# Denominators that leave PSUM group by group, four PSUM banks used in turn, and an order chosen among ten

## The chip, the cores and the metric

The kernel runs on one core of one Trainium2 chip. The metric is the device time of one execution in microseconds (us). The kernel before took 819.15, 821.52 and 824.37 us in three executions; their median is 821.52 us. A further execution was profiled; its own time stands in the table below.

## The reference

The computation is one pre-norm layer over `x` of 4 batches, 512 tokens and 1024 features, in float32:

```
h    = layernorm(x)
q    = h @ Wq                         # 32 heads of 32
k, v = split(h @ Wkv)                 # one key head and one value head for all 32 query heads
s    = q k^T / sqrt(32) + slope[head] * (key - query), causal
x    = x + softmax(s) v @ Wo
w    = (unpack6(qweight) - zero_point) * scale          # 1024 x 1024, four 6-bit codes per 3 words
x    = x + layernorm(x) @ w^T + bias
```

Softmax is computed as exp(s - max) with the products against the values first and the division by the sum of the exponentials (the denominator) later.

## The kernel before

**Tiling.** The 32 heads are taken as 8 groups of 4 heads, for each of 4 batches: 32 steps. A step of the attention runs through these stages; the names in quotes are the tiles that the profile prints.

- `queries` (matmuls on L703 into "pq"): 24 matmuls of 512 columns; the weights and the normalised input are split into a high and a low part, so three products per chunk. ScalarE copies the high part "qh", VectorE subtracts to get the low part "ql", both go through DRAM ("q_d") and come back stacked by head in "qs", of which there are three buffers.
- `maxima` (L762 into "s", two PSUM banks): scores with queries on partitions; VectorE takes each row's maximum (L778, "junk", "mx"). The maxima are transposed ("trm", L794), split ("mt") and sent by DMA into two rows of "qs".
- `attention` (L846 into "st", two PSUM banks): scores with keys on partitions, the maximum already subtracted by the extra rows; ScalarE exponentiates out of PSUM (L856, "p"), GpSimd clears what lies above the diagonal (L865). The products with the values (L875, "pav") and the denominators (L904, "den") are matmuls of 32 output columns, four of them side by side in the array (`tiled=True` for the planner). Before the denominators GpSimd adds the later key blocks of "p" onto the first (L887). "pav" is copied out by ScalarE (L893, "a") and stored to DRAM ("at_d").
- The denominators of the 8 groups of a batch are added into one PSUM tile "den" with a selecting weight "onesel", so that group g stands in row g of each head's 32 partitions. After the eighth group `invert` (L916) takes the reciprocal of the whole tile in four VectorE instructions and four DMAs store it ("rden_d").

**Afterwards**, for 16 tiles of 128 tokens: "raw" (products and reciprocals fetched from DRAM, multiplied on GpSimd, L1051), the output projection (L1074, "po", 48 matmuls of 512 columns per tile), residual, layernorm, a transposition, and the feed-forward product (L1194, "pf", 32 matmuls per tile). In between, `unpack` turns the packed weights into codes: for each of 8 row blocks a load ("qw"), three VectorE instructions, a transposing DMA and a store.

**PSUM.** There are eight banks: two for "s", two for "st", and one each for four pools. "av" holds "pav", "den" the denominators of a batch, "q" the queries, and "misc" the transposed inputs "tr", the keys and values "pkv", "trkv" and "trm". Towards the end "q" and "misc" also serve "po", "pf" and "tr" of the first token tiles.

**What sets the order.** Nothing is issued as it is written down. Each operation is recorded with an engine, a cost, a due time `at` and the items it reads and writes. `Work.slots` gives each new tile of a pool the buffer whose last use is due first, and adds the edges that follow from the reuse. `Work.forward` then lays all operations out in time, engine by engine, with fixed latencies (`LAT`: the time from the end of an operation until another engine sees it), `Work.backward` derives when each is wanted, and `Work.order` repeats this (four rounds of six passes), keeping the order whose end comes first. The instructions of TensorE, ScalarE, VectorE, GpSimd and the DMA queue of SyncE (SP) stand in that order in the program; each queue is served strictly in order, so an instruction that waits holds all behind it. The token tiles (`token_tile`) and the reuse of "q" and "misc" there are part of the same plan.

## Time and profile before

| | |
|---|---|
| profiled execution: its own time / its span | 821.6 us / 819.6 us |
| median of the three runs | 821.52 us (819.15 to 824.37) |
| TensorE (PE) busy | 796.1 us, 97% |
| PE weight loads (PEld) busy | 592.9 us, 72% |
| VectorE (DVE) busy | 563.6 us, 69% |
| GpSimd (POOL) busy | 520.2 us, 63% |
| ScalarE (ACT) busy | 378.3 us, 46% |
| mean granted PE clock | 0.997 |
| chain that ended last | PE 89%, DVE 4%, ACT 2%, DMA 2%, POOL 2%, issue 1% |
| matmuls recorded: L703 pq / L1074 po / L1194 pf | 768 / 768 / 512, of 512 columns |
| L904 den | 256 records, 33.9 us |
| L916 reciprocals | 16, 937 ns each |
| L893 copy of "pav" | 32, 588 ns each |

The span is the time from the first to the last profiled instruction; some 2 us of the execution lie around it. A PE that is called busy can still lose time: matmuls are pipelined and overlap in the records, so what a matmul costs is read from the distance between the starts of neighbours, not from its own duration. Idle time of an engine is listed with what ended it.

### The profile page before, as it was taken

To read this page: it belongs to the slowest core of one execution; us is meant where nothing else is said; L and a number is where in the kernel's file an instruction comes from. 1 tells how busy PE (TensorE), PEld (TensorE's weight loads), DVE (VectorE), ACT (ScalarE), POOL (GpSimd) and SP (SyncE) were. 2 spreads that over 40 slices of the span, in tenths; PEclk is the share of its full clock that TensorE was granted. 3 is DMA by queue.
4 is the path that set the end of the run, shared out by engine and by line. 5 is a ranking of instruction groups with operands and counts; after the bars stand their busy time and mean duration, and the time that the engine had idled before them with its cause. 6 is when DMAs were issued, how large, how long until landed. Compare 5 with 4: busy or idle time off the path is not lost.

```text
span 819.6 us, 13342 instructions
## 1 busy us (share of the span) xinstructions
PE 796.1 (97%) x4464; PEld 592.9 (72%) x4464; DVE 563.6 (69%) x1496; ACT 378.3 (46%) x669; POOL 520.2 (63%) x442
## 2 busy tenths in 40 slices
PE   5999999999899999999999999999999999999997
PEld 5767666777566777666777677667888888888886
DVE  7576776478767278678457776644997686667755
ACT  5644754655665544786555574340142322323320
POOL 5239876556857554797289997878556444545623
PEclk9999999999999999999999999999999999999999
DMA  7277642566733576954659775446985565567311
GB/s 228 64 178 201 191 140 72 153 186 188 231 91 88 156 198 198 263 148 106 198 166 265 205 224 172 159 108 141 245 183 142 144 166 130 131 142 174 103 39 64
DMA packets 130355, 130.76 MB, mean 160 GB/s; under 512 B 42804, under 2 KB 92980, under 8 KB 129264
## 3 DMA queue, kind: packets, MB, share of 16 engines
q1 hardware_dynamic: 129472, 126.39, 56.0%
q0 software_dynamic: 816, 3.53, 1.6%
q8 instruction: 35, 0.57, 0.3%
q14 instruction: 32, 0.26, 0.1%
HBM read 84.01 MB, written 38.80 MB: 150 GB/s over the span
## 4 chain that ended last, share of the span: by engine, by line
PE 89%; DVE 4%; ACT 2%; DMA 2%; POOL 2%; issue 1%; DVEq 0%; POOLq 0%
PE po L1074 21%; PE pq L703 19%; PE pf L1194 14%; PE st L846 9%; PE s L762 9%; PE pav L875 8%; PE den L904 4%; DVE junk L778 2%; PE tr L602 2%; PE pkv L620 2%; POOL p L887 1%; DMA wo_st<-in_L_attn_Wo_dram 1%; ACT p L856 1%; DVE qs L684 1%; DMA x<-_attn_hidden_states_dram 0%
## 5 line engine op out<-in xcount | busy, mean ns | idle before, releaser
L778 DVE CUSTOM_DVE_ANT_0 junk<-s,mask 128x384 f32<-128x384 f32 (+3 forms) x512 | 250.3, 489 | 118.3 <-PE s L762 90.3
L887 POOL TENSOR_TENSOR p<-p,p 128x1536 f32<-128x1536 f32 (+2 forms) x96 | 231.6, 2412 | 18.7 <-PE pav L875 16.9
L856 ACT ACTIVATE p<-st 128x512 f32<-128x512 f32 (+1 forms) x352 | 184.8, 560 | 111.4 <-PE st L846 99.8
L703 PE MATMUL pq<-xc,wqh 128*128 128x512 f32 x512 | 198.3, 403 | 0.2
L1074 PE MATMUL po<-woh,aT 128*128 128x512 f32 x512 | 166.3, 391 | 0.0
L865 POOL TENSOR_SCALAR_AFFINE_SELECT p<-p 128x512 f32<-128x512 f32 x128 | 83.9, 660 | 117.8 <-ACT p L856 116.3
L762 PE MATMUL s<-kst,qs 124*128 124x384 f32 (+3 forms) x512 | 128.3, 325 | 6.4 <-DVE mx L778 3.1
L846 PE MATMUL st<-qs,kst 126*128 126x512 f32 (+1 forms) x352 | 128.2, 401 | 2.0 <-ACT p L856 1.7
L762 PEld LDWEIGHTS s<-kst,qs 124*128 124x128 f32 x512 | 91.6, 189 | 43.4 <-DVE mx L778 12.5
L1194 PE MATMUL pf<-wf,xT 128*128 128x512 f32 x512 | 121.4, 390 | 0.0
L1074 PEld LDWEIGHTS po<-woh,aT 128*128 128x128 f32 x512 | 96.1, 188 | 21.4 <-ACT a L893 0.8
L703 PEld LDWEIGHTS pq<-xc,wqh 128*128 128x128 f32 x512 | 96.9, 189 | 19.8 <-DVE ql L418 1.0
L1194 PEld LDWEIGHTS pf<-wf,xT 128*128 128x128 f32 x512 | 95.9, 188 | 20.5 <-issue 0.6
L703 PE MATMUL pq<-xc,wql 128*128 128x512 f32 x256 | 100.9, 394 | 0.0
L1074 PE MATMUL po<-wol,aT 128*128 128x512 f32 x256 | 99.7, 390 | 0.0
L846 PEld LDWEIGHTS st<-qs,kst 126*128 126x128 f32 x352 | 63.8, 190 | 23.5 <-ACT p L856 9.4
L875 PE MATMUL pav<-p,kv 128*32 128x512 f32 (+3 forms) x1024 | 79.7, 436 | 0.0
L1214 POOL TENSOR_TENSOR x<-x,y 128x512 f32<-128x512 f32 x30 | 44.6, 1486 | 45.9 <-DVE y L1205 45.8
L875 PEld LDWEIGHTS pav<-p,kv 128*32 128x32 f32 x1024 | 29.6, 109 | 48.3 <-issue 36.7
L1074 PEld LDWEIGHTS po<-wol,aT 128*128 128x128 f32 x256 | 48.1, 188 | 9.4
L703 PEld LDWEIGHTS pq<-xc,wql 128*128 128x128 f32 x256 | 48.9, 191 | 6.1
L1172 POOL TENSOR_TENSOR x<-x,rows 128x512 f32<-128x512 f32 x32 | 41.6, 1320 | 16.9 <-issue 8.5
(91 smaller groups left out, 847.0 us busy)
## 6 DMA issues: line engine op xcount, KB each, us to landing
qs<-q_d SPq DMA_DIRECT2D x90, 256.0 KB
x<-_attn_hidden_states_dram SPq DMA_DIRECT2D x31, 512.0 KB
at_d<-a SPq DMA_DIRECT2D x32, 256.0 KB
raw<-at_d SPq DMA_DIRECT2D x16, 512.0 KB
raw<-rden_d SPq DMA_DIRECT2D x64, 128.0 KB
out_dram<-x SPq DMA_DIRECT2D x32, 256.0 KB
q_d<-qh SPq DMA_DIRECT2D x30, 256.0 KB
q_d<-ql SPq DMA_DIRECT2D x30, 256.0 KB
```

The lines of the kernel that those rows point to most:

```text
L703: nc.tensor.matmul(pq(), w()[:, c, :], xc[b, c]()[:, s, :], start=(c == 0 and n == 0), stop=(c == KC - 1 and n == 2),)
L762: nc.tensor.matmul(ps()[:, o : o + W], q()[0:R_MAX, at, ts(t, P)], k()[0:R_MAX, :W], start=True, stop=True,)
L778: lambda ps=ps, junk=junk, t=t, h=h, W=W, o=o: nc.vector.tensor_tensor_reduce(out=junk()[:, :W], in0=ps()[:, o : o + W], in1=mask()[:, S - ...
L846: nc.tensor.matmul(ps()[:, place, :], k()[0:R_ALL, ts(j, P)], q()[0:R_ALL, mine, j * P :], start=True, stop=True,)
L856: lambda ps=ps, own=own, j=j: nc.scalar.activation(pr[j]()[:, own, :], ps(), AF.Exp),
L865: nc.gpsimd.affine_select(out=d, in_=d, pattern=[[0, GH], [1, P]], compare_op=ALU.is_ge, fill=0.0, base=0, channel_multiplier=-1,)
L875: nc.tensor.matmul(pav()[ts(h, HD), j * P :], kv[b]()[:, j, :], pr[j]()[:, h, :], start=(j == 0), stop=(j == NT - 1), tile_position=(0, h ...
L887: nc.gpsimd.tensor_tensor(d, d, pr[j](), ALU.add)
L1074: nc.tensor.matmul(po(), aT[s][1]()[:, c, :], w()[:, ts(n, HALF)], start=(c == 0 and m == 0), stop=(c == KC - 1 and m == 2),)
L1172: nc.gpsimd.tensor_tensor(d, d, rows["bias"][n][1](), ALU.add)
L1194: nc.tensor.matmul(pf(), xT()[:, s, c, :], wf[c]()[:, ts(n, HALF)], start=(c == 0 and s == 0), stop=(c == KC - 1 and s == 1),)
L1214: (nc.vector if last else nc.gpsimd).tensor_tensor(d, d, y(), ALU.add)
```

## The change

Five things are changed, all in one step.

1. **The denominators of a group get a tile of their own.** The four matmuls use an all-ones weight "ones" and start and stop in one go; ScalarE copies the tile to SBUF (pool "stg"), and a DMA stores one row per head (4 rows of 512) to "den_d". The planner's due time of the matmuls is 20 instead of 25 us after the group's start.
2. **The inversion goes through DRAM.** For a batch, a DMA fetches all denominators as 128 x 128 into "rec", one VectorE instruction inverts them, and one DMA stores them to "rden_d". There were four VectorE instructions and four DMAs.
3. **One PSUM pool "m" of four banks** takes the place of "av", "den", "q" and "misc".
4. **The planner.** `LAT` is 40 ns longer for four engines. `order` makes ten plans: the first from the due times as given, nine with a random shift of each due time (standard deviation 0.3 us). Each is laid out again by `replay`, in the fixed order, with 20 ns more latency and at two settings of DMA rate and latency, and the plan with the smallest sum of the two ends is taken. `plan` (the former `order`) also keeps the edges that belong to its best order.
5. **`unpack`** is due at other times: three blocks near the start of batch 1, three near the start of batch 2, two near the start of batch 3 (before: evenly from 7.6 steps on, every 2.6 steps).

The diff, cut to its core:

```diff
-    LAT = {"PE": 310, "ACT": 230, "DVE": 230, "POOL": 230, "SP": 0}
+    LAT = {"PE": 350, "ACT": 270, "DVE": 270, "POOL": 270, "SP": 0}
...
+    def replay(self, line, late, rate, dma_lat):
+        n = len(self.ops)
+        seen, mine = [0.0] * n, [0.0] * n
+        free = dict.fromkeys(self.ENGINES, 0.0)
+        dma = port = 0.0
+        tiled = False
+        for o in line:
+            t = free[o.eng]
+            for m in o.before:
+                a = self.ops[m]
+                t = max(t, mine[m] if a.eng == o.eng and not a.size else seen[m])
+            if o.size:
+                free[o.eng] = t + self.ISSUE[o.eng]
+                dma = max(dma, free[o.eng]) + o.size / rate
+                seen[o.n] = dma + dma_lat
+                continue
...
+            seen[o.n] = t + o.cost + o.lat + late
+        return max(seen)
...
+    def order(self, plans=10, spread=0.3):
+        at = [o.at for o in self.ops]
+        own = [o.before for o in self.ops]
+        best = None
+        for n in range(plans):
+            rnd = random.Random(n)
+            for o, a, b in zip(self.ops, at, own):
+                o.at, o.before = a + (rnd.gauss(0.0, spread) if n else 0.0), dict(b)
+            line = self.plan()
+            end = sum(self.replay(line, *m) for m in SLOWER)
+            if best is None or end < best[0]:
+                best = (end, line, self.end, [o.before for o in self.ops])
...
+SLOWER = ((20.0, 265.0, 2000.0), (20.0, 280.0, 2600.0))
...
-    for name, bufs in (("s", 2), ("st", 2), ("av", 1), ("den", 1), ("q", 1), ("misc", 1)):
+    for name, bufs in (("s", 2), ("st", 2), ("m", 4)):
...
-        if g == 0:
-            den[b] = new("ps_den", "den", [P, S], F32, f"den_{b}")
-        d = den[b]
+        d = new("ps_m", "m", [P, S], F32, f"den_{i}")
...
-                    d()[ts(h, HD), :], onesel()[:, g, :], pr[0]()[:, h, :],
-                    start=(g == 0), stop=(g == NG - 1), tile_position=(0, h * HD),
+                    d()[ts(h, HD), :], ones(), pr[0]()[:, h, :],
+                    start=True, stop=True, tile_position=(0, h * HD),
                 )
-        pe(at + 25.0, [4.0 * S], sums, [d], [pr[0]], tiled=True)
+        pe(at + 20.0, [4.0 * S], sums, [d], [pr[0]], tiled=True)
+        kept = new("stg", "stg", [P, S], F32, f"d_{i}")
+        act(at + 25.5, S, lambda: nc.scalar.copy(kept(), d()), [kept], [d])
+        dma(
+            at + 26.0, 8e3,
+            lambda: nc.sync.dma_start(out=den_d[b, :, g, :], in_=kept()[0:P:HD, :]),
+            [(den_i[b], g)], [kept],
+        )
...
-        for t in range(NT):
-            work.op(
-                "DVE", at + 0.1 * t, 840.0,
-                lambda t=t: nc.vector.reciprocal(r()[:, ts(t, P)], d()[:, ts(t, P)]),
-                [(r, t)], [d],
-            )
-        for h in range(GH):
-            dma(
-                at + 1.0, 16e3,
-                lambda h=h: nc.sync.dma_start(out=rden_d[b, h], in_=r()[h * HD : h * HD + NG, :]),
-                [(rden_i[b], h)], [r],
-            )
+        r = new("rec", "rec", [P, P], F32, f"rec_{b}")
+        dma(
+            at, 65e3,
+            lambda: nc.sync.dma_start(
+                out=r(), in_=den_d[b].rearrange("h g (c q) -> (h g c) q", q=P)
+            ),
+            [r], [den_i[b]],
+        )
+        work.op(
+            "DVE", at + 2.5, 840.0, lambda: nc.vector.reciprocal(r(), r()), [r], [r],
+        )
+        dma(
+            at + 4.0, 65e3,
+            lambda: nc.sync.dma_start(
+                out=rden_d[b].rearrange("h g (c q) -> (h g c) q", q=P), in_=r()
+            ),
+            [rden_i[b]], [r],
+        )
...
-        unpack(T0 + (7.6+2.6*c) * STEP, c)
+        unpack(T0 + (NG*(1+c//3)+.8+1.2*(c%3)) * STEP, c)
```

## The prediction

> **What bounds the kernel now.** I read the page first, then the table of 20 us stages, the chain that ended last, the waits of TensorE, and at the places they named the timeline. The page:
>
> ```profile
> span 819.6 us, 13342 instructions
> ...
> PE 796.1 (97%) x4464; PEld 592.9 (72%) x4464; DVE 563.6 (69%) x1496; ACT 378.3 (46%) x669; POOL 520.2 (63%) x442
> ...
> PE   5999999999899999999999999999999999999997
> ```
>
> The reader is to see that no other engine is near its limit, and that TensorE is busy in every slice but the first and last. The chain tells what a matmul costs when nothing disturbs it:
>
> ```profile
> 589.37 21.76 PE po L1074 x96
> 611.13 7.25 PE pf L1194 x32
> ```
>
> 21.76 / 96 = 7.25 / 32 = 0.227 us per 512 columns. From the distances between starts in the same trace, 384 columns take 0.173, 256 take 0.117, 128 take 0.058 us, a transposition 0.112, a group's products ("pav") 2.15 and its denominators ("den") 0.86. All matmuls at these prices: 2464 of 512 columns, 559.3; 256 of 384, 44.3; 128 of 256, 15.0; 128 of 128, 7.4; 32 groups at 3.01, 96.3; 160 transpositions, 17.9; the small ones 2.9; together 743 us. The span is 819.6, so 77 us are not matmul work: 7.9 before the first matmul, 4.8 from the start of the last one to the end, some 14 for 124 turns between the four-in-one matmuls and the others, and about 50 for waits. From 575 to 800 us there are none (PE 20.00 of 20.00 us in each stage). So the change can only act on small waits in the first 575 us. The waits of TensorE's two queues name the loops:
>
> ```profile
> PEld s L762 <- DVE mx L778: 12.5, 22, 1.6
> PEld st L846 <- ACT p L856: 9.4, 23, 0.9
> ```
>
> (Columns: total us, places, longest.) These are the two-bank loops: a score bank waits for VectorE's maximum, a transposed-score bank for ScalarE's exponential. The largest single wait is of another kind:
>
> ```profile
> 224.41 0.48 PE L762 MATMUL s<-kst,qs 124*128 124x512 f32 x1 [1.54 <-DMA q_d<-ql]
> ```
>
> and what surrounds it, as stages (PE, PEld, DVE, ACT, POOL busy; granted clock; DMA share; GB/s):
>
> ```profile
> 207.00:210.00 3.00, 1.85 (x8) 1.24 (x8) 1.56 (x6) 1.09 (x2) 3.00 (x3) 1.00 0.95 349
> ...
> 222.00:224.00 2.00, 0.87 (x3) 0.39 (x3) 1.61 (x5) 1.78 (x4) 2.00 (x3) 1.00 0.81 272
> 224.00:226.00 2.00, 1.59 (x6) 1.28 (x7) 0.92 (x3) 0.49 (x1) 2.00 (x4) 0.69 0.04 13
> 226.00:228.00 2.00, 2.00 (x6) 1.62 (x6) 0.76 (x3) 0.81 (x3) 0.10 (x1) 0.50 0.02 4
> ```
>
> PE waited, and the granted clock then fell to a half: 2 x 0.31 + 2 x 0.50, and 2 x 0.04 in the next stage, 1.7 us lost. At 208.6 us PE lost 1.3 us at the first score matmul of group 13 while the DMA engines were 95% busy.
>
> **The change, part by part.** The built programs give each engine's order. I priced TensorE's order with the prices above and took, for each PSUM bank, the spacing: the TensorE work between the last matmul of one tile in a bank and the first of the next. Setting the spacings of before against the trace's starts tells what a short one costs; the spacings of the changed order then give the rest.
>
> 1. *Score banks.* Before, 12 spacings under 1.2 us cost 3.1 us, 1.2 of it one place in the opening, so 0.17 for each of the others. The new order has 9. Three fewer: **-0.5**.
> 2. *Transposed-score banks.* Before, 20 spacings under 0.8 us: 3 under 0.2 cost 1.66, 1 under 0.4 cost 0.15, 8 under 0.6 cost 1.79, 8 under 0.8 cost 0.69, together 4.3. The new order has 0, 2, 6 and 7, at the same means 0.3 + 1.3 + 0.6 = 2.3: -2.0. Between 0.8 and 1.4 us 132 places become 120, at 0.02: -0.2. **-2.2**.
> 3. *The four shared banks.* Spacings under 2 us fall from 28 to 10. Before, the waits at such places were 1.14 (tr, four), 1.04 (pq, six), 0.39 (trm, two) and 0.40 (pkv), 2.97 in all. Of the new ten two are shorter than what empties the bank: 0.39 us after a "tr" (ScalarE 0.596 and VectorE 0.685 must come first: 0.9 short) and 0.56 after a "den" (0.588 and a signal: 0.15 short). 1.1 remains: **-1.9**.
> 4. *The stack "qs"* has three buffers: from the last transposed score of group i-3 to the first score of group i its reload must fit. Before, the tightest spacing was 5.4 us (group 13, the wait of 1.3), so 6.7 was needed; group 14 lost 1.7 to the late "ql" above. The new order has 5.4 and 5.9 (groups 22 and 21), short by 1.3 and 0.8: 2.1 against 3.0, **-0.9**. If no wait of that length is left in one piece, the clock's fall goes too: **-1.7**.
> 5. *Denominators, ScalarE.* 32 copies like the one of "pav":
>
> ```profile
> L893 ACT COPY a<-pav 128x512 f32<-128x512 f32 x32 | 18.8, 588 | 36.2 <-PE pav L875 34.0 <-issue 1.2 <-ACT p L856 0.7
> L916 DVE RECIPROCAL rec<-den 128x128 f32<-128x128 f32 x16 | 14.7, 937 | 1.5 <-PE den L904 1.3 <-issue 0.2
> ```
>
>    18.8 us more on ScalarE. What hides them is its idle time, 10 of 20 us in most attention stages; queued behind a copy are exponentials, and PE waits for those. In the new order no copy stands ahead of an exponential whose scores come earlier. Bounds: 0, and 18.8 if every one delayed PE. ScalarE has 2% of the chain, 16 us for its 378 busy: 18.8 x 16 / 378, **+0.8**.
> 6. *Inversion, VectorE.* 16 instructions of 0.937 become 4 of 128 x 128: 11.2 us less, of which those of batches 0 to 2 stood at 188-195, 303-312 and 440-448 us, two of these in stages where VectorE is 17.1 and 17.6 of 20 us busy. Bounds: 0 and -11.2; "junk", 2.5% of the chain or 20 us, in 320 us of VectorE time before 560 us: 11.2 x 20 / 320, **-0.7**. The new fetch, inversion and store for batch 0 come some 45 us of TensorE work ahead of the first "po", those of the others during the token tiles; each is off the path unless two DMA trips outlast that.
> 7. *SP's queue* gets 32 small stores, 4 fetches, and 4 stores for 16. Before, such an issue takes about 0.33 us (four stores of "rec": 1.30). No "qh", "ql" or "mt" store stands behind a denominator store whose copy comes later. 0, at most 32 x 0.33 = 10.6 were each in front of a late "qs".
> 8. *Denominator matmuls* stay 128, same size. Turns rise from 124 to 130: a "den" takes 1.00 us after a turn and 0.86 without, and 0.97 until a following score matmul where 0.86 would do: three pairs of 0.14 + 0.11, **+0.75**.
> 9. *Unpacking* moves no work on or off an engine; its loads and code stores come further from the "x" loads that stood in the pile-up of 205-210 us. Counted in 4.
>
> Sum: -0.5 - 2.2 - 1.9 - 0.9 - 1.7 + 0.8 - 0.7 + 0.75 = -6.35. The profiled execution took 821.6 us (819.6 and 2.0 around it), 0.1 over the median of the three runs: **815.2 us**, 0.8% less. About 1%, 8.2 us, is what a measurement here tells from no change.
>
> *Two rules weighed.* The Trainium skill, page "TensorE: Matmul & The Clock Gate", section "HAM oscillation — how this bites in real kernels", warns of idle gaps over about 3.4 us as what makes the clock fall; here 1.54 us of idle preceded the fall (stages 222-228), so trace and rule differ in size. By the rule the 1.7 us would not hang on that wait, and the sum would be 816.9. The same section reports a kernel in which PSUM double-buffering "gave no further gain". By that part 3 would be worth nothing and the sum would be 817.1; the waits of 2.97 us at such places speak for the smaller spacing.
>
> **Rivals.**
> - *The gains return elsewhere* (0.25): the waits are a few tenths each at some 80 places; one that goes lets PE arrive earlier at the next DMA or GpSimd step. For it: at 523-540 us PE loses 2.4 us to GpSimd's adds (L887), which nothing here shortens; against it: the spacings grow in three kinds of bank at once. Parts 1 to 4 halved, no clock gain, 5 to 8 as they are: 821.6 - 2.8 + 0.85, 819.7.
> - *The order removes more than the short spacings* (0.19): the latencies are 40 ns longer in the plan, and every score loop gains. PE's waits above 0.06 us at "s", "st" and the transpositions, without the opening, are about 25 us; were half of it gone, with the clock's 1.7 and +0.85: 821.6 - 13.4, 808. Against it: two-bank spacings under 1.4 us fall only from 186 to 155.
> - *Slower, by the stack's reload* (0.10): spacings of 5.4, 5.9, 6.8 and 7.2 us at groups 22, 21, 27 and 28. If the DMA trips there take 9.5 us rather than 6.7, the waits are 4.1 + 3.6 + 2.7 + 2.3 = 12.7 in place of 3.0, each of the two pairs followed by a fall of the clock (3.4 in place of 1.7), against -3.75 from parts 1 to 3 and 5 to 8: 821.6 + 9.7 + 1.7 - 3.75, 829.3. It decides from 7.6 us on (2.2 + 1.7 + 0.8 + 0.4 = 5.1 in place of 3.0, and the falls). For it: DMA shares of 0.95 at 207-210 and 1.02 at 340-344; against it: before, group 12 had 6.4 us and did not wait.
> - *The ten plans differ in nothing the chip sees*: then the result is the first rival's.
>
> **How the numbers follow.** Forecast 0.46 (811 to 819), gains returned 0.25 (819 to 824), more 0.19 (803 to 811), slower 0.10 (824 to 835). 804 to 826 leaves out the far ends of the last two, and takes in the copies at a third of their bound. Faster by over 1% (under 813.3): 0.19 and a third of the forecast's 0.46, 0.35. Slower by over 1% (over 829.7): 0.08, the upper half of the last case and a little for the bounds of parts 5 and 7. Within: 0.57.
>
> **What would show it.** The changed profile should have PE near 790 us busy with the same matmul counts; fewer places and less time for "s" on "mx" and "st" on "p"; 4 reciprocals; ScalarE near 397; no half-clock stage between 100 and 560 us. Waits on "copy of den", on "q_d" or "qs" DMAs at groups 21, 22, 27 or 28, or a half clock there, would show the forecast wrong, and so would an unchanged count of waits.

## The result and the profile after

Four executions of the changed kernel have a median of 831.19 us (831.15 to 832.63); the kernel before, beside it, 821.01. The ratio is 1.0124, with a 95% interval of 1.0089 to 1.0159: **1.2% slower**, where 815.2 us and no more than 826 were forecast. The profiled execution took 831.19 us, its span is 829.5. The page of the kernel after:

```profile
span 829.5 us, 13448 instructions
...
PE 799.8 (96%) x4464; PEld 593.4 (72%) x4464; DVE 578.2 (70%) x1484; ACT 396.3 (48%) x701; POOL 519.3 (63%) x434
...
PE   4999989999999999999999999998899999999997
```

ScalarE rose by the 18 us of the copies, as forecast. VectorE should have fallen by 11 us and rose by 15. TensorE has two slices of 8 around 560 to 600 us, where it had only nines before. The same groups as before, with their new line numbers:

```profile
L942 ACT COPY a<-pav 128x512 f32<-128x512 f32 x32 | 18.9, 591 | 31.7 <-PE pav L924 25.4 <-POOL wol L540 2.6 <-ACT d L958 1.9
L958 ACT COPY d<-den 128x512 f32<-128x512 f32 x32 | 18.8, 588 | 18.7 <-PE den L951 17.7 <-DMA at_d<-a 0.6
...
L976 DVE RECIPROCAL rec<-rec 128x128 f32<-128x128 f32 x4 | 3.8, 945 | 2.3 <-DMA rec<-den_d 2.3
```

Of the two-bank loops "s" waits as much as before and "st" 2.0 us less (total us, places, longest), and a new wait stands beside them:

```profile
PEld s L812 <- DVE mx L828: 12.6, 27, 1.3
...
PEld st L895 <- ACT p L905: 7.4, 19, 0.8
...
DVE rows L1073 <- DMA rows<-n_weight_zero_point_dram: 6.5, 1, 6.5
```

To find where the 9.9 us of span went, I put TensorE's starts against the prices of the prediction once more: each distance between neighbouring starts, less the price of the earlier one and less 0.105 us for a turn. What is left over is wait (a half clock counts as wait here).

| us of wait between | 0-60 | 60-460 | 460-545 | 545-600 | sum |
|---|---|---|---|---|---|
| before | 12.1 | 32.7 | 7.0 | 0.2 | 52.0 |
| after | 13.2 | 33.8 | 4.0 | 8.9 | 59.9 |

With 1.0 us of a later first matmul (7.92 to 8.95 us) and 0.6 us for six more turns, the 7.9 make 9.5 of the 9.9. So beside this one profile of the kernel before the attention stages are 1.9 us better, the opening costs 2.1 with the late start, and **the handover from the attention to the token tiles costs 8.7 us, in a stretch in which the prediction had seen no wait at all.** The 1.9 are not safe. The run e19 below has the kernel before's instructions in the same order up to 460 us, and its profile shows 29.3 us of wait from 60 to 460 in place of 32.7: the wait at 224 us and the half clock behind it did not come. Beside that profile the changed kernel's attention stages are 1.5 us worse. The handover, 0.2 before, is 8.9 in either case.

The largest piece of the handover in the stages (length; PE, PEld, DVE, ACT, POOL busy; granted clock; DMA share; GB/s):

```profile
576.00:578.00 2.00, 1.97 (x9) 1.31 (x7) 0.00 (x0) 0.00 (x0) 0.46 (x1) 1.00 1.03 175
578.00:580.00 2.00, 0.00 (x0) 0.00 (x0) 0.00 (x0) 0.00 (x0) 0.00 (x0) 1.00 1.03 247
...
582.00:584.00 2.00, 1.21 (x7) 1.22 (x7) 2.00 (x4) 0.00 (x0) 1.19 (x1) 0.74 1.15 161
584.00:586.00 2.00, 2.00 (x7) 1.71 (x7) 2.00 (x4) 1.07 (x2) 2.00 (x2) 0.50 0.82 193
```

All five engines stand still at 578 to 580 us while the DMA engines are full; the half clock follows. TensorE's wait ends with the transposition of token tile 2 (its timeline):

```profile
582.79 1.84 PE L1168 MATMUL tr<-ident,x 128*128 128x128 f32 x8 [4.82 <-DVE x L1155]
```

By the distance between starts it is 4.98 us. The chain of waits tells what they stand still for (start, us, what):

```profile
554.48 5.60 DVE aT L469
...
562.07 6.33 DMA raw<-rden_d
...
570.91 3.48 POOL x L1231 x2
574.40 6.90 DMA rows<-n_weight_zero_point_dram
...
581.93 0.82 DVE x L1155
582.74 0.04 issue
582.79 1.84 PE tr L1168 x8
```

Read from below: the transpositions of token tile 2 need "x2" (L1155), which stands in VectorE's queue behind the preparation of the zero-point rows (L1073); the rows' load took 6.90 us and was issued by GpSimd only at 574.40, behind bias additions (L1231) and the multiplication of tile 3's "raw" (L1111); that waited for the divisors, whose load could start only when VectorE's subtraction for tile 2 (L469) was done, and this subtraction took 5.6 us where the shortest of its kind in this trace takes 1.15.

In the kernel before the same loads were issued at 566.20 and 569.57. How near it was to the same wait is in its VectorE and TensorE timelines:

```profile
570.61 0.69 DVE L1013 SCALAR_TENSOR_TENSOR rows<-rows,scale_qh 128x512 f32<-128x512 f32 x1 [0.70 <-DMA rows<-n_weight_zero_point_dram]
...
572.72 0.81 DVE L1095 TENSOR_SCALAR x<-x,mv_f,rstd_f 128x1024 f32<-128x1024 f32 x1
```

```profile
574.95 1.03 PE L1109 MATMUL tr<-ident,x 128*128 128x128 f32 x8
```

"x2" was finished at 573.53 and its transposition began at 574.95. The stage had no wait, but only 1.4 us in hand.

### The profile page after: what moved, and what is told of

Its sections match the earlier page's. It is cut to its first block, busy times and chain, and to the rows that moved or that the text cites. A ratio compares the mean times of both kernels' runs of the same rounds, so it can differ in the third digit from the quotient of the medians.

```text
span 829.5 us, 13448 instructions
## 1 busy us (share of the span) xinstructions
PE 799.8 (96%) x4464; PEld 593.4 (72%) x4464; DVE 578.2 (70%) x1484; ACT 396.3 (48%) x701; POOL 519.3 (63%) x434
## 4 chain that ended last, share of the span: by engine, by line
PE 87%; DVE 4%; DMA 4%; issue 1%; ACT 1%; SPq 1%; POOL 1%; DVEq 0%; ACTq 0%; POOLq 0%
PE pq L753 20%; PE po L1134 19%; PE pf L1253 14%; PE s L812 9%; PE st L895 9%; PE pav L924 8%; PE den L951 3%; PE pkv L670 2%; DVE junk L828 2%; PE tr L652 1%; DMA rows<-n_weight_zero_point_dram 1%; DMA wq_st<-in_L_attn_Wq_dram 1%; DMA raw<-rden_d 1%; DMA qs<-mt 1%; DMA qs<-qr_d 1%
## 5 line engine op out<-in xcount | busy, mean ns | idle before, releaser
L828 DVE CUSTOM_DVE_ANT_0 junk<-s,mask 128x128 f32<-128x128 f32 (+3 forms) x512 | 250.9, 490 | 111.3 <-PE s L812 84.0
L895 PE MATMUL st<-qs,kst 126*128 126x512 f32 (+1 forms) x352 | 130.8, 400 | 0.7 <-DMA qs<-mt 0.5
L1231 POOL TENSOR_TENSOR x<-x,rows 128x512 f32<-128x512 f32 x32 | 44.6, 1414 | 16.7 <-DVE x L1155 11.1
```

The costliest lines, as they stand in the source:

```text
L828: lambda ps=ps, junk=junk, t=t, h=h, W=W, o=o: nc.vector.tensor_tensor_reduce(out=junk()[:, :W], in0=ps()[:, o : o + W], in1=mask()[:, S - ...
L895: nc.tensor.matmul(ps()[:, place, :], k()[0:R_ALL, ts(j, P)], q()[0:R_ALL, mine, j * P :], start=True, stop=True,)
L1231: nc.gpsimd.tensor_tensor(d, d, rows["bias"][n][1](), ALU.add)
```

## The experiments

All times are medians. The ratio, which lies near that of the means, is against executions of the kernel before on the same chip (medians of 818.9 to 820.3 us); in e1 one execution of 842.49 us lifts it, and by medians it is 1.014. Waits come from each kernel's one profile by the method above. "longest aT" is the longest VectorE subtraction L469 of the turned attention.

| run | us | ratio (95%) | waits 0-60, 60-460, 460-545, 545-600 | longest aT, us |
|---|---|---|---|---|
| before | 821.01 | 1 | 12.1, 32.7, 7.0, 0.2 | 2.35 |
| after | 831.19 | 1.0124 (1.0089-1.0159) | 13.2, 33.8, 4.0, 8.9 | 5.58 |
| e1_rows | 831.15 | 1.0172 (1.0105-1.0239) | 12.5, 32.8, 4.0, 10.0 | 5.60 |
| e2_rows_x1 | 830.42 | 1.0144 (1.0117-1.0171) | 12.8, 32.7, 4.0, 8.3 | 5.60 |
| e3_opening | 831.46 | 1.0137 (1.0095-1.0179) | 9.9, 33.6, 12.4, 7.8 | 10.66 |
| e4_copies | 832.56 | 1.0164 (1.0138-1.0189) | 12.9, 34.1, 4.2, 10.4 | 5.61 |
| e6_rows_load | 831.78 | 1.0137 (1.0056-1.0219) | 12.8, 33.0, 12.4, 7.7 | 10.62 |
| e7_plan0 | 825.18 | 1.0043 (1.0010-1.0075) | 9.5, 33.7, 4.6, 7.3 | 8.85 |
| e8_planner_only | 832.32 | 1.0147 (1.0081-1.0213) | 14.2, 29.8, 10.6, 3.6 | 3.15 |
| e9_old_planner | 839.95 | 1.0231 (1.0156-1.0306) | 9.0, 39.4, 5.8, 10.8 | 9.67 |
| e10_port | 834.43 | 1.0197 (1.0146-1.0248) | 13.9, 34.3, 5.1, 10.7 | 6.59 |
| e11_aT_pool | 843.15 | 1.0295 (1.0278-1.0311) | 13.7, 34.0, 16.6, 6.5 | 2.44 |
| e12_aT_rows | 840.04 | 1.0253 (1.0234-1.0271) | 13.6, 32.8, 16.7, 7.3 | 2.43 |
| e14_plan0_aT | 832.49 | 1.0168 (1.0147-1.0188) | 9.6, 32.7, 16.4, 2.8 | 1.23 |
| e15_gaps | 832.08 | 1.0153 (1.0132-1.0175) | 12.9, 35.4, 5.6, 7.7 | 3.52 |
| e16_gaps_rows | 829.67 | 1.0125 (1.0100-1.0150) | 11.2, 32.7, 5.6, 5.4 | 3.35 |
| e17_plan0_gaps | 819.38 | 1.0002 (0.9991-1.0013) | 10.0, 32.6, 4.4, 2.3 | 3.55 |
| e18_all | 823.61 | 1.0046 (1.0031-1.0062) | 9.4, 32.7, 5.2, 3.8 | 3.35 |
| e19_before_gaps | 826.06 | 1.0073 (1.0053-1.0094) | 11.7, 29.3, 8.8, 4.8 | 3.68 |
| e20_planner_rows_gaps | 840.09 | 1.0249 (1.0233-1.0266) | 14.3, 31.0, 11.2, 9.8 | 4.05 |

e8, e9 and e20 have another 4 us of waits behind 600 us; the others at most 0.8.

### One place in a queue at a time (e1 to e4)

```diff
     ordered = work.order()
+    ordered.remove(mark["zs", 0])                       # L1073, first half
+    ordered.insert(ordered.index(mark["x2", 2]) + 1, mark["zs", 0])   # e1: behind L1155 of tile 2
...
+    ordered.remove(mark["x1", 2])                       # e2: also the residual load of tile 2 ...
+    ordered.insert(min(ordered.index(o) for o in mark["raw", 3]), mark["x1", 2])   # ... ahead of tile 3's
```

> The changed kernel with its order kept, but for one move on VectorE: the scaling of the zero-point rows (L1073, first half) goes behind the normalisation of token tile 2 (L1155), in front of which it stood. Theory A: this scaling waits 6.45 us for its load and holds tile 2's normalisation, so PE's wait of 4.98 us at 582.8 us and the half clock after it (1.7 us) come from this place in the queue. By A both go, the waits of 545 to 600 us fall from 8.9 to 2 or 3 us and the time from 831.2 to about 824.7. Theory B: the late load of the residual for tile 2 behind tile 3's loads in SP's queue (VectorE waited 8.28 us for it) sets the time and the rows wait beside it. By B the time stays within 1 us of 831.2. Theory C: the copies of the denominators and the turns cost the time everywhere; by C also no change here.

> As the run before, and on SP the load of tile 2's residual (L1125) goes ahead of the five loads of tile 3. Theory A: the move on VectorE has taken nearly all; this one takes the remaining 1 us (waits of 0.4 and 0.7 us at 572 to 573 us): about 823.7. Theory B: the gain of some 7 us comes with this move and not before: about 824 here and 831 in the run before.

831.15 and 830.42 us: neither move gives the time back, so theory A fails in both, and so does theory B of the second. The wait only changed its place. In e1 the transposition no longer waits, but the feed-forward product behind it does (TensorE's timeline), because its "xT" is subtracted on VectorE behind the same rows:

```profile
585.87 4.63 PE L1259 MATMUL pf<-wf,xT 128*128 128x512 f32 x10 [4.06 <-DVE xT L469]
```

In e1 the rows land at 580.63 us and in the kernel after at 581.29: the products wait for them wherever VectorE uses them.

```diff
     ordered = work.order()
+    opening = [...]            # 109 operations of the first 22 us, in the order of the kernel before
+    mine = iter([next(o for o in ordered if o.n == n) for n in opening])
+    ordered = [next(mine) if o.n in set(opening) else o for o in ordered]
```

> The changed kernel with its order kept, but the operations of the first 22 us stand in the order of the kernel before (109 of them, on all engines). Theory A: of the 9.9 us lost, 2.1 are lost by 60 us, since the last normalised tile comes at 16.0 instead of 14.1 us and PE gets its full clock at 23.3 instead of 16.5 us. By A PE's opening is that of before, full clock near 16.5 us, and the time falls by 2.1 to about 829.1. Rival: later waits in the first groups (VectorE's subtractions and maxima at 30 to 45 us) take the gain back: 831 and the same place at 60 us.

The opening came back: first matmul at 8.10 us, waits before 60 us 9.9 in place of 13.2. The time did not (831.46). TensorE, by the starts of the same matmuls 4.4 to 5.1 us ahead of the kernel after until 467 us, lost all of it at 494 us, where its next scores waited 6.18 us for a maximum that stood in VectorE's queue behind a subtraction of token tile 1 (VectorE's timeline):

```profile
483.14 10.66 DVE L469 TENSOR_TENSOR aT<-raw,aT 128x1024 fp32r<-128x1024 f32 x1
```

That is the same line as in the chain above, again far over its 1.15 us. GpSimd worked without a pause from 479 to 492.7 us.

```diff
-        act(at + 25.5, S, lambda: nc.scalar.copy(kept(), d()), [kept], [d])
+        def copies():
+            nc.scalar.copy(kept(), d())
+            nc.scalar.copy(kept(), d())
+        act(at + 25.5, S, copies, [kept], [d])
```

> The changed kernel with its order kept and each of the 32 copies of the denominators made twice in a row (the second writes the same values), 18.8 us more on ScalarE. Theory A: these copies lie in ScalarE's idle time; as in the prediction 18.8 us of them cost about 0.8 us: 832. Theory C: a copy holds the exponentials and the layernorm of the next batch behind it on PE's path (as at 102 to 105 us); then each costs a tenth of a us or more, 3 to 6 us in all, 834 to 837, and as much of the loss is theirs.

832.56 us: 18.8 us more of ScalarE cost 1.4 by the medians, not 3 to 6. By the starts of the same matmuls it is at most 0.8 us behind the kernel after through the attention, and 0.3 at its end; the last 1.5 come at the handover, where the half clock of e4's profile lasts 6.8 us in place of 3.4. So the copies are not where the time went, and 0.8 was the right size for them.

### The row loads, and the parts of the change (e6 to e9)

```diff
+    last_add = next(o for o in work.ops if o.n == mark["add"])        # last L936
+    for o in mark["load"][3:]:                                        # the two loads of zero-point rows
+        ordered.remove(o)
+    at = ordered.index(last_add) + 1
+    ordered[at:at] = mark["load"][3:]
```

> The kernel after with its order kept, except that GpSimd issues the two loads of the zero-point rows (L1061) right after its last addition of exponentials (L936), some 559 us into the span instead of 574.4 behind six bias additions and a multiplication (L1231, L1111). Theory A (the 4.98 us wait of TensorE at 582.8 and the half clock behind it hang on these loads landing at 581): the rows land near 566-567, VectorE's L1073 does not wait, TensorE's waits of 545-600 us fall from 8.9 to about 2, and the time falls by 4.98 + 1.7 = 6.7 us from 831.2 to 824.5. Rival B (the handover is late for other reasons too, as the runs with the moved instruction on VectorE and the earlier x load hint): a wait of 3 us or more comes at another tile within 15 us, and the time stays within 829 to 833.

831.78 us, with a wide spread (827.94 to 837.48; the profile is of the slowest). The wait on the rows is gone; in the profile two others stand for it, 6.3 us at 498 and 3.4 us at 583, both behind stretched subtractions (10.62 and 5.58 us). Rival B, but the new waits have one kind of cause. How far the faster executions share them is not shown.

> The kernel after with the first of the ten plans in place of the chosen one; everything else of the change is kept. Theory R (the gain and the loss come with the buffers and the added instructions): the waits by stage look like the kernel after's, within 3 us in all, and the time is 828 to 834. Theory P (it is this particular order that loses, at its two ends): the waits before 60 us and of 545-600 us fall from 13.2 and 8.9 to near 12 and 2 or less, and the time is 820 to 824.

The edit is `work.order(plans=1)`. 825.18 us, between the two theories: same buffers, same copies, same inversion, and 6 us less from taking the first plan. So the plan that the kernel chose among its ten is not the best of them on the chip. What is left to lose here is one wait on the same kind of instruction (VectorE's and TensorE's lines of the timeline):

```profile
551.63 8.85 DVE L469 TENSOR_TENSOR aT<-raw,aT 128x1024 fp32r<-128x1024 f32 x1
...
560.54 0.76 PE L1134 MATMUL po<-woh,aT 128*128 128x512 f32 x2 [4.47 <-DVE aT L469]
```

```diff
-    LAT = {"PE": 310, "ACT": 230, "DVE": 230, "POOL": 230, "SP": 0}
+    LAT = {"PE": 350, "ACT": 270, "DVE": 270, "POOL": 270, "SP": 0}      # e8: in the kernel before, with
...                                                                       # replay, plan, order, SLOWER
```

> The kernel before, its PSUM banks, denominators and inversion as they were, with the new latencies of the plan (40 ns longer) and the best of ten plans. Theory R (buffers): the time stays within 819 to 823, and the waits from 60 to 545 us stay near 39. Theory P (the planner): the wait on the zero-point rows or one like it shows here too, the waits of 60-545 us fall by the few us that the transposed-score banks gained in the kernel after, and the time lies 3 us or more off the kernel before, on either side.

```diff
-    LAT = {"PE": 350, "ACT": 270, "DVE": 270, "POOL": 270, "SP": 0}
+    LAT = {"PE": 310, "ACT": 230, "DVE": 230, "POOL": 230, "SP": 0}      # e9: in the kernel after
...
-    ordered = work.order()
+    ordered = work.order(plans=1)
```

> The kernel after's four shared banks, copied denominators and batched inversion, with the old latencies and a single plan. Theory R (buffers): 828 to 834, with the late first normalised tile (first matmul 8.9 us in the span) and a wait of 3 us or more between 575 and 600 us. Theory P (planner): 820 to 824. If both halves carry a share, this run and the one with the planner alone lie between 823 and 828, or the two differences from the kernel before add to about 10 us.

832.32 and 839.95 us. The planner alone loses 1.5%, the buffers with the old latencies lose 2.3%, both together 1.2%: the halves do not add. Neither the buffers nor the planner is "the" cause: the four new plans measured so far (the kernel after, e7, e8 and e9) place the work of 460 to 600 us in four ways, and all four are slower than the kernel before. The new due times of `unpack` went with the buffers (they are in e9 and not in e8) and were not tried alone. In e9 the subtraction took 9.67 us and TensorE waited 6.75 for it at 566 us.

### What stretches the subtraction (e10)

In the kernel after, VectorE's instruction ends 1.09 us after GpSimd's first pause, which is about its own length. Beside GpSimd, whose row from 554.10 to 558.98 has no gap:

```profile
554.10 2.40 POOL L936 TENSOR_TENSOR p<-p,p 128x1024 f32<-128x1024 f32 x1
556.45 1.28 POOL L1273 TENSOR_TENSOR x<-x,y 128x512 f32<-128x512 f32 x1
557.71 1.28 POOL L936 TENSOR_TENSOR p<-p,p 128x512 f32<-128x512 f32 x1
560.75 1.29 POOL L1273 TENSOR_TENSOR x<-x,y 128x512 f32<-128x512 f32 x1 [1.77 <-DVE y L1264]
```

stands VectorE:

```profile
553.88 0.69 DVE L1264 TENSOR_TENSOR y<-pf,scale_qh 128x512 f32<-128x512 f32 x1 [3.83 <-PE pf L1253]
554.48 5.58 DVE L469 TENSOR_TENSOR aT<-raw,aT 128x1024 fp32r<-128x1024 f32 x1
559.99 1.27 DVE L1264 TENSOR_TENSOR y<-pf,scale_ql 128x512 f32<-128x512 f32 x2
```

L1264 reads one operand from PSUM and takes its 0.69 us beside a busy GpSimd; L469 here reads both from SBUF. To see whether GpSimd is what it waits for, GpSimd got more to do:

```diff
         for o in ordered:
             o.fn()
+            if o.n == mark["add"]:                       # last L936
+                for _ in range(2):
+                    nc.gpsimd.tensor_tensor(idle(), idle(), idle(), ALU.add)   # 128 x 512
```

> The kernel after with two additions of a 128 x 512 tile of its own (about 1.28 us each, nobody reads them) issued by GpSimd right after its last addition of exponentials (L936, ends at 559.0 us in the profile after), ahead of GpSimd's first pause there. Theory A (a VectorE instruction whose operands are all in SBUF waits for GpSimd's first pause): the subtraction of tile 2's turned attention, 128 x 1024 at L469, which took 5.58 us from 554.48 and ended 1.07 us after GpSimd's last instruction, takes 5.58 + 2.5 = 8.1 us and again ends 1.1 us after GpSimd stops. Theory B (something else, such as its own operands or a DMA, stretches it): it stays at 5.6 us. The time is 1 to 3 us over the kernel after's by A, the same by B.

```profile
556.96 6.59 DVE L469 TENSOR_TENSOR aT<-raw,aT 128x1024 fp32r<-128x1024 f32 x1
...
560.18 1.28 POOL L939 TENSOR_TENSOR p<-p,p 128x512 f32<-128x512 f32 x1
...
561.42 1.03 POOL L1360 TENSOR_TENSOR idle<-idle 128x512 f32<-128x512 f32 x1
```

The second added addition follows in the same timeline:

```profile
562.53 1.91 POOL L1360 TENSOR_TENSOR idle<-idle 128x512 f32<-128x512 f32 x1
```

The subtraction took 6.59 us, neither 5.6 nor 8.1. The reason is in the starts: the second addition needs the first, so GpSimd paused from 562.45 to 562.53 us, 0.08 us, and VectorE ended at 563.55, 1.10 us after the beginning of that pause; the second addition took 1.91 us where the first took 1.03. So the subtraction waits for GpSimd, as theory A has it, and then runs its 1.1 us in one go while GpSimd waits; a pause of 0.08 us is enough. But a pause is not always needed. In the kernel before a subtraction got in between two GpSimd instructions that follow without one (GpSimd's timeline, then VectorE's), and the second of them took 1.65 us, a microsecond more than the 0.64 of its kind elsewhere:

```profile
549.89 1.31 POOL L1214 TENSOR_TENSOR x<-x,y 128x512 f32<-128x512 f32 x1
551.15 1.65 POOL L865 TENSOR_SCALAR_AFFINE_SELECT p<-p 128x512 f32<-128x512 f32 x1
```

```profile
550.97 1.34 DVE L418 TENSOR_TENSOR aT<-raw,aT 128x1024 fp32r<-128x1024 f32 x1
```

The 20 profiles hold 74 of these subtractions (for "aT") that took over 1.3 us. Each ended 1.07 to 1.10 us after the end of a GpSimd instruction. On the way they met 121 such ends. Where a pause or the issue of a DMA followed, 28 times, the subtraction always got in; where the next GpSimd instruction followed at once, 93 times, it got in 46 times and 47 times not. What decides there is not shown: the same pair of GpSimd instructions, the addition of 128 x 1536 and the mask behind it, let it in at 490.28 us in the kernel after and not at 491.80 in e10.

The Trainium skill, page "SBUF — State Buffer", section "Who interferes with whom", has the rule that fits: a VectorE instruction with two SBUF inputs contends with a GpSimd instruction that reads SBUF, and the one that comes first holds the shared port for the whole instruction. By that rule the wait would be over with the GpSimd instruction that was running, some 2 us at 554.48; here it outlasted a row of three, and of six in e7. That the next GpSimd instruction can go ahead of a VectorE instruction that already waits, about every second time, is what these runs add.

### Taking the stretch away (e11 to e18)

```diff
+        if k < 3:
+            work.ops[-1].fn = lambda: nc.gpsimd.tensor_tensor(        # was nc.vector
+                aT[1][1](), raw[0][1](), aT[0][1]().bitcast(F32), ALU.subtract
+            )
...
+    for k in range(3):                     # one GpSimd instruction behind the multiplication L1111
+        times, high, low = mark["aT", k]
+        ordered.remove(low)
+        at = ordered.index(times)
+        at = next(i for i, o in enumerate(ordered) if i > at and o.eng == "POOL")
+        ordered.insert(max(at, ordered.index(high)) + 1, low)
```

> The kernel after's order, with the subtraction of the turned attention (L469 for aT) of tiles 0, 1 and 2 done by GpSimd itself, one GpSimd instruction after the multiplication that feeds it, and not by VectorE. Theory A (the stretch of that subtraction behind GpSimd's row of work delays the handover): tile 2's is done at 556.5 and not at 560.06 us, the divisors of tile 3 are loaded some 3 us earlier, and of TensorE's 4.98 us wait at 582.8 about 1.5 stay and the half clock goes: 831.2 - 3.5 - 1.7 = 826. Theory B (the handover is held by the two row loads alone): it stays at 830 to 833.

> The two earlier edits together: GpSimd does the subtraction of tiles 0 to 2, and issues the two loads of zero-point rows right after its last addition of exponentials. Theory A (the wait of the handover has two causes in a row, each of which shows the other when it is taken away alone; with the row loads moved alone the subtraction took 10.62 and 5.58 us and two waits of 6.3 and 3.4 us came): neither wait is left, the waits of 545-600 us fall from 8.9 to about 2, and those of 460-545 us stay near 4: 831.2 - 6.7 = 824.5. Rival B (a third cause stands behind these two): a wait of 2 us or more between 575 and 600 us, 828 to 832.

> The kernel after with the first of the ten plans, which took 825.2 us and whose largest wait, 4.64 us at 560.5 with a half clock of 3.4 us behind it, followed a subtraction L469 of 8.85 us; here GpSimd does that subtraction for tiles 0 to 2. Theory A: the wait and the half clock go, 4.6 + 1.7 = 6.3 us less, 819 us, which is the kernel before's time. Theory B (the wait is held by what comes ahead of the multiplication, not by VectorE): 824 to 827.

843.15, 840.04 and 832.49 us (e12 also moves the row loads, e14 uses the first plan). A mistake of mine hides what they were made for: tile 0's target buffer still held codes that a DMA was storing, and GpSimd, now at that place, waited (its timeline in e11), and with it the masks (L915) that TensorE needed, for 10.84 us, followed by 10 us of half clock:

```profile
468.77 2.34 POOL L1127 TENSOR_TENSOR aT<-raw,aT 128x1024 fp32r<-128x1024 f32 x1 [11.28 <-DMA wf_d<-codes]
```

On VectorE the subtraction stood later, and in the kernel after it waited only 0.26 us for that store. Only the third tells something behind it: in e14 the waits of 545 to 600 us are 2.8, where e7 with the same plan has 7.3.

So the engine was left as it was, and GpSimd got gaps instead:

```diff
+    gaps = set()
+    for k in (1, 2):
+        after = ordered[ordered.index(mark["times", k]) + 1 :]
+        gaps |= {o.n for o in [o for o in after if o.eng == "POOL" and not o.size][:4]}
...
         for o in ordered:
             o.fn()
+            if o.n in gaps:
+                for _ in range(2):                      # the second needs the first
+                    nc.gpsimd.tensor_tensor(tiny(), tiny(), tiny(), ALU.add)   # 128 x 8
```

> The kernel after's order; after each of the four GpSimd instructions that follow the multiplication of tiles 1 and 2 (L1111), GpSimd does two additions of a 128 x 8 tile of its own, of which the second needs the first (nobody else reads them). In the run with two added additions a pause of 0.08 us between two such dependent instructions was followed by the end of the VectorE subtraction 1.09 us later. Theory A (any gap of GpSimd lets the waiting VectorE instruction in): the subtraction of tile 2 takes 2 to 3.5 us in place of 5.58, that of tile 1 under 3; the rows come 2 to 3 us earlier at most, since GpSimd issues their loads behind the multiplication of tile 3: 827 to 830. Theory B (gaps of that size do not let it in): 5.6 us again, 831 to 834.

> The same gaps, and GpSimd issues the two loads of zero-point rows right after its last addition of exponentials. Theory A (two causes, the rows and the stretched subtractions, each of which shows when the other is taken away): the 6.3 us wait at 498 and the 3.4 us wait at 583 of the run with the row loads moved alone are gone, the waits of 460-545 us are near 4 and those of 545-600 us 1 to 3: 822 to 826. Rival B (a third cause): a wait of 2 us or more between 570 and 600 us, 828 to 832.

> The kernel after with the first of the ten plans (825.2 us; 4.64 us of wait at 560.5 with a half clock of 3.4 us behind it, after a subtraction of 8.85 us), with the same gaps. Theory A: the subtraction takes 2 to 3.5 us, the wait falls to under 1 us and the half clock goes: 825.2 - 4 - 1.7 = 819.5. Theory B: 824 to 827.

> The kernel after with its first 109 operations in the order of the kernel before, the row loads moved and the gaps. Theory A (what the change lost, it lost at its two ends; the middle gained about 2 us): waits of about 10 before 60 us, 38 from 60 to 545 us, 2 behind it, no half clock: 742.2 + 13.65 + 50 + 8.1 + 4.8 + 2 = 820.8, the kernel before's time within 2 us. Rival B (what is taken away in one place returns in another): 826 or more.

- e15: the gaps shorten one subtraction, but the time does not move (832.08). The subtraction of tile 2, from VectorE's timeline:

```profile
557.41 1.22 DVE L469 TENSOR_TENSOR aT<-raw,aT 128x1024 fp32r<-128x1024 f32 x1
```

  5.58 became 1.22 us (tile 1's did not: 3.52 after 3.37), and TensorE still waited 4.23 us at 584.5 for "x2" behind the rows, whose load was now issued at 576.71. The stretch alone is not the cause under this plan.
- e16, with the row loads moved as well: 829.67 (the profile is of the fastest, 826.88), worse than the 822 to 826 expected by A. The two waits of e6 are gone; what is left between 545 and 600 us, 5.4, begins where tile 3's first products wait for GpSimd's multiplication. By the profile GpSimd's queue is a third cause in the row, as rival B had it; no run takes it away.
- e17, the first plan with the gaps: **819.38 us, 1.0002 of the kernel before (0.9991 to 1.0013)**, as theory A had it (819.5). The 8.85 us became 3.55, the 4.47 us wait of TensorE and the half clock are gone. By the starts of the same matmuls 4.7 us are won there; 1.1 more come before 460 us, where e7's profile has a half clock of 3.4 us at 70 us and this one has none. TensorE's timeline:

```profile
567.02 0.50 PE L1138 MATMUL po<-woh,aT 128*128 128x512 f32 x1 [0.80 <-ACT aT L466]
568.28 0.74 PE L1138 MATMUL po<-woh,aT 128*128 128x512 f32 x2 [0.53 <-DVE aT L469]
```

  The pause between the two small additions was not what let the subtraction in here. It got in one step earlier, behind the addition of exponentials and ahead of the first small one, so that the pair took 1.48 us in place of some 0.48 (GpSimd's timeline, then VectorE's):

```profile
550.12 2.41 POOL L939 TENSOR_TENSOR p<-p,p 128x1024 f32<-128x1024 f32 x1
552.48 1.48 POOL L1358 TENSOR_TENSOR tiny<-tiny 128x8 f32<-128x8 f32 x2
```

```profile
550.08 3.55 DVE L469 TENSOR_TENSOR aT<-raw,aT 128x1024 fp32r<-128x1024 f32 x1
```

  So e17 shows that breaking up GpSimd's row takes most of the stretch, and the wait behind it, away, not that the pause as such did it.
- e18, the chosen plan with the old opening, early rows and gaps: 823.61, 7.6 us less than the kernel after, still 0.5% over the kernel before. In its profile no half clock is left between the opening and the end. Three edits stand in it together; no run says what each is worth there.

### The same gaps in the kernel before (e19, e20)

> The kernel before with the same gaps of GpSimd behind the multiplication of tiles 1 and 2, everything else kept. The change with the first plan and these gaps took 819.4 us against 819.5 of the kernel before. Theory A (before, no stretched subtraction stands on the path: its longest is 2.35 us at 565): within 818 to 821, and then the buffers and the batched inversion are worth nothing when the stretch is out of the way on both sides. Rival B (the kernel before loses to the stretch too, in its 7 us of waits between 460 and 545 us): 814 to 817, and then the buffers cost some 3 us.

> The kernel before with the new planner alone (832.3 us), with the row loads issued right after GpSimd's last addition of exponentials, and the gaps. Theory A (the planner loses at the same handover): the waits behind 545 us, 3.6 + 4.1 there, fall to 3 or less and a half clock goes: 825 to 828. Rival B (its losses lie at many places, in the opening and at 460 to 545 us): 830 or more.

Neither theory of e19: 826.06 us, 0.7% slower. What moved first is small. In the kernel before, VectorE's subtraction began at 564.99 us, just behind the start of a GpSimd addition, and waited for it:

```profile
564.98 1.27 POOL L1214 TENSOR_TENSOR x<-x,y 128x512 f32<-128x512 f32 x1
```

```profile
564.99 2.35 DVE L418 TENSOR_TENSOR aT<-raw,aT 128x1024 fp32r<-128x1024 f32 x1
```

In e19 it began just ahead of the same addition, which now waited for it:

```profile
564.80 1.23 DVE L418 TENSOR_TENSOR aT<-raw,aT 128x1024 fp32r<-128x1024 f32 x1 [1.50 <-ACT aT L415]
```

```profile
564.90 2.28 POOL L1218 TENSOR_TENSOR x<-x,y 128x512 f32<-128x512 f32 x1
```

So GpSimd issued the first row load at 567.13 in place of 566.20, and SP, which waits for the subtraction, sent the next loads of "raw" from 566.06 on and not from 567.36. The row load, ahead of them before, now stood behind them. It took 6.29 us, where VectorE had it 4.4 us after its issue in the kernel before; at 568 to 570 us the DMA share was now 1.14, and 0.70 before. The chain of waits of e19:

```profile
567.13 6.29 DMA rows<-n_weight_zero_point_dram
...
573.45 0.69 DVE rows L1016
```

TensorE's transposition of tile 2 then waited, in its timeline,

```profile
576.43 1.97 PE L1113 MATMUL tr<-ident,x 128*128 128x128 f32 x8 [3.09 <-DVE x L1099]
```

and the half clock of 3.4 us followed. **0.9 us of delay in GpSimd's queue, and 1.9 us more for a load that had lost its place ahead of others, turned the unchanged kernel into one with the changed kernel's wait.**

The other profiles fit. This row load took 5.8 to 7.3 us in ten of the 20, the kernel after among them, and in each of these SP had issued a load of "raw" at most 0.5 us before it. In the other ten, the kernel before, e7 and e17 among them, the last such issue was 3.4 us or more before, and it took 3.7 to 5.0 us. No run moves this order alone.

e20 (840.09) is the planner alone with both edits and is worse than without them; TensorE waited 4.97 us at 582 for GpSimd's multiplication, so GpSimd's queue has no room for the gaps there. Why the planner alone loses 3.6 us at 460 to 545 us stays open.

## Why the prediction was wrong

1. **The step that failed** is the reading "From 575 to 800 us there are none. So the change can only act on small waits in the first 575 us." A stage without waits was taken for a stage with reserve. "x2" was 1.4 us early there, and the change moved the loads ahead of it from 566.20 and 569.57 us to 574.40. There they stood behind loads of "raw" and took 6.90 us, where the first had taken 4.4; "x2" came at 582.7, and TensorE waited 4.98 us, with a half clock behind it. GpSimd's queue was not looked at; part 7 asked this question for SP's queue alone. The 8.7 us of this stretch, which the sum puts at nothing, are most of the result.
2. **Part 6**, the inversion on VectorE, -0.7: the reciprocals fell by 11 us as said, but VectorE's time rose by 15, since an instruction that waits for GpSimd counts as busy. By summed durations the zero-point products (L1235) take 10.1 us more, the unpacking's "v" 8.3, the subtractions for "aT", "xT" and "kst" 4.4, 3.5 and 3.4, less 8.5 in two other groups, all of them on SBUF; "junk", "ql" and "y", which read PSUM, are the same within 0.6. So part 9, which moved the unpacking at no cost, was not free on VectorE either. The stretched ones of the zero-point products and of "xT" all end 0.55 us after the end of a GpSimd instruction, those of "v" 0.25 to 0.29, as those of "aT" end 1.07 to 1.10 after one. A mean duration hid that an "aT" subtraction takes 1.15 or 5.6 us, by what GpSimd does beside it.
3. **Parts 1 and 3**, score banks -0.5 and shared banks -1.9: not found. From 60 to 545 us the waits at "s" are 14.1 us after 13.3, though the two places at 208 and 224 us that held 3.0 of them are gone; those at "tr", "pq", "trm" and "pkv" 14.4 after 13.9. Longer spacings did not help because the waits that took their place are not waits for a bank but for what VectorE or a DMA delivers: 1.05 us for "mx" at 116.3 ("trm"), 0.89 for "mx" at 288, 0.52 for "qs" at 320.9, 0.54 for "qs" at 451.
4. **Part 2**, transposed-score banks, -2.2: held, 8.2 us became 4.9, -3.3 (in e19's profile, which has the kernel before's order up to 460 us, the 8.2 are 0.8 less).
5. **Part 4**, the stack: the 1.3 us at 208 and the half clock at 226 are gone; at 320.9, 365 and 451 us some 2.0 remain, 2.1 were put there. But the change need not have taken the second one away: e19 has the same order of instructions there, and in its profile TensorE waits 1.2 us at 208 and does not wait at 224, and the clock does not fall. The -1.7, and group 14's 1.7 in the 3.0, were priced from something that does not come in every execution. The mean granted clock says the same: 0.997 in the profiled execution, 0.999 or 1.000 in 25 of the 57 executions of the kernel before beside the experiments, where a half clock of 3.4 us would take 0.002. These 25 have a median of 818.9 us, and the forecast started from 821.6. The slower rival built on the stack did not come; that the outcome is near its 829.3 is chance.
6. **Part 5**, ScalarE's copies, +0.8: the doubling of the copies cost at most 0.8 in the attention, and 1.4 in the whole. **Part 8**, +0.75: 0.63 by six turns of 0.105.
7. **The opening** was not in the sum: +2.1 us with the later first matmul. e3 shows that it is the order of the first 109 operations, and that the 4.4 to 5.1 us won are given back at 494 us under this plan.
8. **"The ten plans differ in nothing the chip sees"** was wrong: the chosen one and the first are 6.0 us apart, 831.19 and 825.18 (ratios 1.0124 and 1.0043). In `replay` a VectorE instruction with SBUF operands waits until the GpSimd instruction listed before it ends; on the chip it was passed over at 47 of 93 such ends without a pause. The ranking does not see this cost. That this is why it chose badly is not shown.

What the change is worth with the stretch out of the way is told by e17 for one plan: nothing that can be measured (1.0002). Its opening is 2.1 us of wait better and 460 to 545 us 2.6 better; 2.1 are lost at the handover and 0.6 to the turns. From 60 to 460 us it has 32.6 us, as much as the profile of the kernel before (32.7) and 3.3 more than e19's (29.3). Another plan can give another number (e18: 1.0046), and what the kernel before would gain without its own stretches stays open, since e19's edit cost it a new wait. No run here was measurably faster than the kernel before.

## What to carry to other kernels

- A stretch without waits tells nothing of its reserve. Before a schedule is changed, take the last few operations ahead of each handover, on the slow queues above all, and measure how early each was; here it was 1.4 us, and a load that was issued 0.9 us later and took 1.9 us longer used it up. Note too which transfers stand just ahead of a load: something faster elsewhere can put others in front of it.
- When VectorE's time goes up although work was taken from it, compare each group with its shortest instruction, and look at what GpSimd does beside the long ones. A long row of GpSimd instructions without a gap can hold a VectorE instruction with SBUF operands for the whole row; a pair of tiny dependent GpSimd instructions between them shortened that in e15 to e18, if GpSimd's queue has the room, and in e19 it moved the delay into GpSimd's queue.
- One profile is one execution. Before a wait in it is priced, look whether another profile of the same order, or the mean clocks of the other executions, show it too; the largest wait of the kernel before did not come again.
- A reordering planner that is given anything new deals every late stage anew. Take one part of the change under the old order, or several orders with the change, before a part is called good or bad.

## What the runs showed of the hardware that was not expected

- VectorE's 128 x 1024 subtraction with both inputs in SBUF: 1.15 us alone, 5.58, 8.85, 9.67 and 10.66 us behind GpSimd rows without a gap. All 74 that took over 1.3 us ended 1.07 to 1.10 us after the end of a GpSimd instruction. Where a pause followed (0.08 us is enough) they got in there every time, and where none did about every second time.
- A load that spreads 2 KB over 128 partitions (256 KB written) took 3.7 to 5.0 us in ten profiles (4.4 in the kernel before) and 5.8 to 7.3 us in the ten in which 512 or 128 KB loads of "raw" had been issued at most 0.5 us ahead of it (6.90 in the kernel after, where the DMA share was 1.03 to 1.10 from 576 to 582 us).
- The size of a wait does not tell whether a half clock of 3.4 us, 1.7 us lost, follows. After 1.3 and 0.53 us within 1.2 us (at 116 us) it came in e10, e11 and e15 and not in the kernel after, e6 or e16, which have the same order of instructions there; 2.25 us at 665 in e8 brought it, 2.39 at 589 in e8 and 2.85 at 487 in e20 did not.
